# Folded weights dealt product by product into the attention of the first image

## The chip, the cores and the metric

The kernel runs on one core of a Trainium2 chip. The metric is the device time of one execution in microseconds. Before the change three runs took 2604.94, 2607.56 and 2609.03 us; the median is 2607.56 us. Engine names in the profile: PE is TensorE (matrix products), PEld its weight loads, DVE is VectorE, ACT is ScalarE, POOL is GpSimd, SP is the engine whose queue issues most DMAs.

## The reference, cut to what matters

Two layers over 8 images of 512 channels and 32 x 32 points (1024 tokens).

```
# layer 0: group norm, q/k/v, 8 heads of 64 channels
q = fake_quant(q); k = fake_quant(k); v = fake_quant(v)     # 8 bits, one range for all images
w = softmax(einsum('bct,bcs->bts', q * scale, k * scale))
a = einsum('bts,bcs->bct', w, v)
x = x + proj_w @ a + proj_b
# layer 1: group norm, attention with one head of 512 channels
qk = (t @ wq.T + bq) @ (t @ wk.T + bk).T / sqrt(512)
out = softmax(qk) @ (t @ wv.T + bv)
x = x + (out @ wp.T + bp)
```

Layer 1 has only one head, so its four weight matrices can be multiplied in pairs before any image is seen: wq with wk, and wv with wp. The kernel calls this the folding. It saves two of the four products with the tokens of each image. The biases that belong to it are folded along.

## The kernel before, in words

First comes a stage for all 8 images (0 to about 583 us): group norm and the products for q, k and v, written to DRAM, with the minimum and maximum that the quantization needs. Then `attention()` and layer 1 run over the images. `attention()` is a generator that hands out score tiles. A unit `u` is one score tile: image `b`, pair of heads `j` (4 pairs), half of the queries `hf` (2), block of keys `s` (8), so 64 units for each image, 16 for each pair.

For each unit, `scores(u)` makes the score tile `st` on TensorE: two products, one for each head of the pair, each over 64 of the 128 rows of the array, at the same time. ScalarE takes the exponential into `pt`. `ps_s` holds two score tiles, so the products of a tile wait until the exponential of the tile two places before has been taken. `split(u)` then divides `pt` into two float16 parts, `two`: the rounded value (a cast on ScalarE, GpSimd or VectorE) and the difference (VectorE). In the first image every fourth tile is *plain*: its exponential goes to `aside` and stays float32. `over_keys` multiplies the parts with the values (`av`), in four strips of 32 columns that run at the same time; for a plain tile in float32 with the values `vf`, in two strips of 64 columns. `totals` makes the row sums (`sm`) with a matrix of ones. The order on TensorE for four units `u` to `u+3` is: scores of `u+6` and `u+7`; values and sums of `u` and `u+1`; scores of `u+8` and `u+9`; values and sums of `u+2` and `u+3`. Each such round is one step of the generator (`advance()`).

When the last round of a pair's half is done, `finish` copies the values (`ao`) and the sums (`rs`) out of PSUM on ScalarE. After the second half the sums go out by DMA (`apart`), VectorE takes reciprocals (`rcs`), these go to DRAM and back spread over the partitions (`rs_d`, `rs`), and VectorE divides `ao`. There is one buffer for `rs`, so the sums of the next pair are copied after the division of this one. `load_pair` fetches the raw q, k and v of the next pair through two `raw` buffers, and VectorE quantizes them.

`fold()` is a second generator. It makes the folded weights: two times (`wn_h` into `wa`, `wn_v` into `wm`) four output blocks (`e`) of four products (`d`) each, every product 128 x 128 by 128 x 512 in float32, accumulated in one PSUM bank of `ps_o`, which ScalarE copies out. `through(i)` makes the bias column on VectorE (four reductions into `room`, a sum, four widenings into `wide`), `weigh` multiplies it with the weights (`wt_f`, four products 32 wide, then a copy on ScalarE), and `by_channel` gives the column sums (`wc_f`, four products with one column). At the end VectorE makes sums and differences of the blocks of `wa` and `wm`, and `wm` is stored to DRAM (`wm_d`) for the later images. Then the projection's weights (`load_wp`) and the first image's x (`load_x2`, tile `h`, which takes over the buffer of `wn_h`) are loaded.

In the kernel before, a loop over `fold()` decides the order: it adds up a weight for each yield of the folding (4.0 for a block of four products) and a weight for each round of attention, and takes rounds of attention while they are behind in proportion. TensorE thus gets four products in a row, then about two rounds of attention.

On TensorE all products are chained in the order of the program (`mm`, line 206). On the other engines, in this stage, the order within a queue comes from the scheduler of the tile framework; from the first image's projection on (`InOrder.planned`) it is chained as well. An engine works through its queue in order, and so does SP's DMA queue.

Of the kernel before, what the change touches and what calls it, by code (L numbers as in the profile page):

```python
# [15 lines left out]
ALU = mybir.AluOpType  # L16
# [3 lines left out]
B, C, HH, WW = 8, 512, 32, 32  # L20
T = HH * WW
CC = C // P
# [36 lines left out]
def attn_pair_kernel(  # L59
# [101 lines left out]
    def awaits(t):  # L161

        pe.t = max(pe.t, t + 0.1)
# [140 lines left out]
    with ExitStack() as fast:  # L304
        wts = fast.enter_context(tc.tile_pool(name="wts", bufs=1))
        def pair_ps(name):
            return ps_s.tile([P, 2, 512], F32, tag="s", name=name)
# [657 lines left out]
        def attention():  # L965
# [13 lines left out]
            def scores(u):  # L979
                b, j, hf, s = units[u]  # L980
                if hf == 0 and s == 0:
                    settle("qk")
                nm = f"{b}_{j}_{hf}"
                qt, kt, _ = pairs[b, j]
                st = pair_ps(f"st_{nm}_{s}")
                awaits(st_free[-2])
                for i, r in enumerate(HALF):
                    mm(
                        st[:, i, :], lhsT=kt[r, bass.ts(s, P)],
                        rhs=qt[r, bass.ts(hf, 512)], start=True, stop=True,  # L990
                    )
                if u >= 4:
                    need(u - 4)
                if plain(b, s):
                    pt = aside[:, u // 4 % 3].rearrange("p (i k) n -> p i (k n)", i=2)
                else:
                    pt = ptp.tile([P, 2, 512], F32, tag="p", name=f"pt_{nm}_{s}")
                there = act.do(
                    1.12, lambda: act.activation(pt, st, AF.Exp, scale=esc),
                    max(pe.t + 0.25, ready.get(u - 4, 0.0) + 0.1),  # L1000
                )
                st_free.append(there)
                pts[u] = pt, there
# [34 lines left out]
            def over_keys(us):  # L1038
                need(us[-1])
                awaits(ready[us[-1]])  # L1040
                pe.t += 0.12
                for u in us:
                    b, j, hf, s = units[u]
                    if s == 0:
                        avs[b, j, hf] = av_bank(f"av_{b}_{j}_{hf}")
                    if plain(b, s):
                        for i, r in enumerate(HALF):
                            mm(
                                avs[b, j, hf][r, :], lhsT=vfs[j][:, s // 4, r],
                                rhs=parts[u][:, i, :], start=False, stop=(s == NT - 1),  # L1050
                            )
                        continue
                    for w in range(2):
                        for i in range(4):
                            r = slice(i * QUAD, (i + 1) * QUAD)
                            mm(
                                avs[b, j, hf][r, :], lhsT=pairs[b, j][2][:, s, r],
                                rhs=parts[u][:, w, i // 2, :], start=(s == 0 and w == 0),
                                stop=(s == NT - 1 and w == 1),
                            )  # L1060
# [57 lines left out]
            for u in (0, 2, 4):  # L1118
                for i in (u, u + 1):
                    scores(i)  # L1120
                    split(i)
                yield 9.0 if u else 0.0, 0
            for u in range(0, len(units), 4):
                b, j, hf, s = units[u]
                if hf == 0 and s == 0:
                    n = b * PAIRS + j + 1
                    if n < B * PAIRS:
                        pairs[divmod(n, PAIRS)] = load_pair(*divmod(n, PAIRS))
                    settle("qv")

                def two(what, v):
                    if v < len(units):
                        what(v)
                        what(v + 1)

                pe.t += 0.12
                if not late:  # L1140
                    two(scores, u + 6)
                if late:
                    over_keys((u, u + 1))
                    two(scores, u + 6)
                    totals((u, u + 1))
                    over_keys((u + 2, u + 3))
                    totals((u + 2, u + 3))
                    two(split, u + 6)
                    two(scores, u + 8)
                elif dense:  # L1150
                    over_keys((u, u + 1))
                    totals((u, u + 1))
                    two(split, u + 6)
                    two(scores, u + 8)
                    over_keys((u + 2, u + 3))
                    totals((u + 2, u + 3))
                else:
                    over_keys(range(u, u + 4))
                    totals(range(u, u + 4))
                    two(split, u + 6)  # L1160
                    two(scores, u + 8)
                if s == NT - 4:
                    finish(b, j, hf)
                two(split, u + 8)
                pe.t += 0.15
                last = (j, hf, s) == (PAIRS - 1, NH - 1, NT - 4)
                yield 6.0 + (hf == NH - 1 and s == NT - 4), b + last

        xts, sums, wms, wps, mvs = {}, {}, {}, {}, {}

        def load_x2(b, dma):

            xts[b] = l1p.tile([P, CC, T], F32, tag="h", name=f"h2_{b}")
            for hf in range(NH):
                dma(xts[b][:, :, bass.ts(hf, 512)], x_v[b, :, :, bass.ts(hf, 512)])

        def load_wp(b, dma):
            wps[b] = l2p.tile([P, CC, C], F32, tag="sums", name=f"wp0_{b}")
            dma(wps[b], w_sq[WP0])
# [482 lines left out]
        def fold():  # L1662
# [16 lines left out]
            def through(i):  # L1679
                w, _, col = ((NQ1, NK1, V_BQ), (NV1, WP1, V_BV))[i]  # L1680
                z = small.tile([P, CC], F32, tag="z", name=f"z{i}")
                for e in range(CC):
                    dve.tensor_tensor_reduce(
                        room, wn[w][:, e, :], row, 1.0, 0.0, ALU.mult, ALU.add,
                        accum_out=z[:, e : e + 1],
                    )
                dve.tensor_add(z, z, vec[:, col : col + CC])
                widen(wide[:, i], z)

            for i, (rows, lw, rw) in enumerate(((wa_rows, NQ1, NK1), (wm_rows, NV1, WP1))):  # L1690
                through(i)
                for e in range(CC):
                    ps = bank(f"fold_{lw}_{e}")
                    for d in range(CC):
                        mm(
                            ps, lhsT=wn[lw][:, d, bass.ts(e, P)], rhs=wn[rw][:, d, :],
                            start=(d == 0), stop=(d == CC - 1),
                        )
                    act.copy(rows(e), ps.rearrange("p (a n) -> p a n", a=2))
                    yield 4.0  # L1700
            for i, (dst, w) in enumerate(((gb, NK1), (ob, WP1))):
                by_channel, _ = weigh(
                    bank, room, lambda e, w=w: wn[w][:, e, :], wide[:, i], f"f{i}"
                )
                yield 1.0
                tot = by_channel()
                if i == 0:
                    dve.tensor_copy(dst, tot)
                else:
                    dve.tensor_add(dst, tot, vec[:, V_BP : V_BP + CC])  # L1710
            a11, a12, a21, a22, s1, s2, s4 = (wa[:, i] for i in range(7))
            tt(s1, a21, a22, ALU.add)
            tt(s2, s1, a11, ALU.subtract)
            tt(a21, a11, a21, ALU.subtract)
            tt(s4, a12, s2, ALU.subtract)
            (m11, m12), (m21, m22), (v1, v2), (v3, v4) = ([t[:, i] for i in range(2)] for t in wm)
            tt(v1, m11, m12, ALU.subtract)
            tt(v2, m22, v1, ALU.subtract)
# [31 lines left out]


        att = attention()
        A_IMAGE = PAIRS * (NH * NT * 1.5 + 1.0)
        F_FOLD = 4.0 * 8 + 2.0
        F_FIRST = 4.0
        pos, done = 0.0, 0
        dense = True
        late = False

        def advance():  # L1760
            nonlocal pos, done
            step = next(att, None)
            pos, done = (math.inf, B) if step is None else (pos + step[0], step[1])

        def others():
            steps = None
# [5 lines left out]

        folded = 0.0
        for w in fold():
            folded += w
            while pos < (folded - F_FIRST) * A_IMAGE / F_FOLD:
                advance()
        load_wp(0, nc.sync.dma_start)  # L1780
        load_x2(0, nc.sync.dma_start)
        while done < 1:
            advance()

        for _ in range(LEAD):
            advance()
# [370 lines left out]
```

## Time and profile before

| | |
|---|---|
| profiled execution, device time | 2605.78 us |
| its span, from the first to the last instruction | 2604.0 us |
| instructions | 38580 |
| TensorE busy | 2532.2 us, 97% of the span |
| VectorE busy | 1905.0 us, 73% |
| ScalarE busy | 1358.1 us, 52% |
| GpSimd busy | 194.1 us, 7% |
| mean granted TensorE clock | 0.995 |
| folding, first and last product | 583.1 us to 675.4 us |
| projection of the first image, first product | 736.73 us |

The page gives the share of each engine in the whole span; the stage of the first image's attention is some 6% of it. Its timeline lists instructions in order of time, merged where the same operation follows itself: start, duration, engine, line of the kernel, operation, output and inputs, shape, count, and in brackets how long the engine stood idle before it and what ended that. Line 206 is the helper that records every product and line 91 the one that records VectorE and ScalarE work, so the tile names tell the operations apart. Durations of products are those of a pipeline; the steps from start to start tell what TensorE can do.

### The profile page before, as it was taken

What the parts mean: (1) busy time and instruction counts of PE and PEld (TensorE: products, weight loads), DVE (VectorE), ACT (ScalarE), POOL (GpSimd) and SP (SyncE); (2) the same over time, 40 slices, a digit from 0 to 9 for tenths busy, and PEclk for the clock granted to TensorE, in tenths of its full rate; (3) what the DMA queues carried; (4) which work ended last, traced back from release to release, by engine and by line L of the source; (5) the groups of instructions that cost most, each with busy time, mean ns of one, the idle gap of its engine ahead of it and who ended that gap; (6) DMA issues with size and microseconds to landing.
All of it is one profiled execution on the core that took longest, in us unless ns stands there. A gap on an engine that the chain in (4) does not pass through costs nothing.

```text
span 2604.0 us, 38580 instructions
## 1 busy us (share of the span) xinstructions
PE 2532.2 (97%) x15606; PEld 1750.0 (67%) x15606; DVE 1905.0 (73%) x2748; ACT 1358.1 (52%) x1696; POOL 194.1 (7%) x153
## 2 busy tenths in 40 slices
PE   8899999998889999999999999999999999999998
PEld 4688888872236775775677577757766775777687
DVE  7877777668767777877877787778777777775544
ACT  3222222217866674766566566746665665664121
POOL 0000000001110001000100010010001000100000
PEclk9999999999999999999999999999999999999999
DMA  5433333333321223223212322322232123212211
GB/s 183 152 127 122 117 117 118 125 131 104 123 66 54 58 94 115 65 74 112 92 49 75 123 93 63 98 89 79 86 102 98 49 78 118 86 47 88 86 37 38
DMA packets 156012, 243.07 MB, mean 93 GB/s; under 512 B 26544, under 2 KB 93104, under 8 KB 154288
## 3 DMA queue, kind: packets, MB, share of 16 engines
q1 hardware_dynamic: 125264, 182.81, 21.4%
q10 hardware_dynamic: 30560, 57.71, 6.5%
q8 instruction: 124, 2.03, 0.3%
q14 instruction: 64, 0.52, 0.1%
HBM read 153.64 MB, written 86.28 MB: 92 GB/s over the span
## 4 chain that ended last, share of the span: by engine, by line
PE 85%; DVE 4%; ACT 3%; issue 2%; DMA 2%; POOL 0%; SPq 0%; ACTq 0%; DVEq 0%
PE s L206 15%; PE o L206 14%; PE qkps L206 11%; PE pj L206 9%; PE av L206 8%; PE v2ps L206 7%; PE g L206 7%; PE vps L206 5%; PE st L206 4%; PE sm L206 4%; ACT pt L91 1%; PE fold L206 1%; DVE two L91 1%; ACT aside L91 0%; DVE acc L91 0%
## 5 line engine op out<-in xcount | busy, mean ns | idle before, releaser
L91 ACT ACTIVATE pt<-st,esc 128x1024 f32<-128x1024 f32 x496 | 527.0, 1114 | 344.1 <-PE st L206 323.7
L91 DVE TENSOR_TENSOR two<-pt,two 128x1024 f16<-128x1024 f32 x496 | 596.8, 1219 | 134.0 <-POOL two L1021 106.5
L91 ACT CAST two<-pt 128x1024 f16<-128x1024 f32 x358 | 362.2, 1055 | 7.9 <-issue 5.3
L1021 POOL CAST two<-pt 128x1024 f16<-128x1024 f32 x128 | 171.3, 1338 | 1546.2 <-ACT pt L91 769.3
L206 PE MATMUL av<-two,v 128*32 128x512 f16 x3968 | 245.0, 381 | 0.0
L206 PE MATMUL s<-g,h 128*128 128x256 f32 x1024 | 233.4, 380 | 0.0
L206 PE MATMUL pj<-ao,wp 128*128 128x512 f32 x512 | 224.7, 597 | 0.0
L206 PEld LDWEIGHTS s<-g,h 128*128 128x128 f32 x1024 | 193.0, 190 | 30.9 <-issue 4.3
L206 PE MATMUL st<-q,k 64*128 64x512 bf16 x1024 | 163.8, 382 | 25.3 <-ACT pt L91 13.1
L206 PEld LDWEIGHTS <-v 128*32 128x32 f16 x3968 | 91.2, 96 | 136.6 <-issue 63.2
L206 PEld LDWEIGHTS pj<-ao,wp 128*128 128x128 f32 x512 | 96.6, 191 | 122.3 <-issue 112.5
L206 PE MATMUL s<-g,sums 128*128 128x256 f32 x768 | 178.4, 381 | 0.2 <-DVE p L91 0.2
L91 ACT ACTIVATE u_ring<-qkps,qkbt 128x512 f32<-128x512 f32 x89 | 60.8, 684 | 224.3 <-PE qkps L206 224.3
L206 PE MATMUL o<-p,v 128*128 128x256 f32 x768 | 175.2, 382 | 1.0 <-DVE p L91 1.0
L206 PEld LDWEIGHTS o<-p,v 128*128 128x128 f32 x768 | 144.3, 190 | 27.0 <-issue 5.7
L206 PEld LDWEIGHTS s<-g,sums 128*128 128x128 f32 x768 | 144.7, 190 | 24.2 <-issue 4.6
L206 PE MATMUL sm<-two,ones 128*32 128x512 f16 x1984 | 136.7, 381 | 1.8 <-ACT rs L91 1.8
L206 PEld LDWEIGHTS <-k 64*128 64x128 bf16 x1024 | 34.8, 94 | 147.9 <-issue 144.5
L206 PE MATMUL qkps<-half,w_high 128*128 128x512 f32 x480 | 132.6, 399 | 0.0
L206 PE MATMUL qkps<-half,w_low 128*128 128x512 f32 x480 | 131.3, 396 | 0.5 <-DVE half L91 0.5
L206 PE MATMUL qkps<-half,w_mix 128*128 128x512 f32 x480 | 130.5, 394 | 1.1 <-DVE half L91 1.1
L206 PE MATMUL g<-h,wa 128*128 128x256 f32 x512 | 121.2, 385 | 1.6 <-DVE h L91 1.6
(219 smaller groups left out, 3836.2 us busy)
## 6 DMA issues: line engine op xcount, KB each, us to landing
rs<-rs_d SPq DMA_DIRECT2D x80, 256.0 KB
x<-in_x_dram SPq DMA_DIRECT2D x32, 512.0 KB
q_d<-wa SPq DMA_DIRECT2D x32, 512.0 KB
k_d<-wa SPq DMA_DIRECT2D x32, 512.0 KB
raw<-q_d SPq DMA_DIRECT2D x32, 512.0 KB
v_d<-v_ring SPq DMA_DIRECT2D x32, 512.0 KB
raw<-k_d SPq DMA_DIRECT2D x32, 512.0 KB
x_d<-h SPq DMA_DIRECT2D x64, 256.0 KB
```

Source lines behind the costliest of these rows:

```text
L91: ins = self.latest = op(*args, **kw).ins
L206: ins = nc.tensor.matmul(ps, lhsT=lhsT, rhs=rhs, **kw).ins
L1021: copy(two[:, 0], pt)
```

## The change

The products of the folding are dealt singly. `fold()` now yields after every product instead of after every block of four, and `scores(u)` takes one step of it ahead of each odd unit of the first image. Nine steps (two blocks and one product) run before the attention begins. The loop with its weights is gone, and the generators yield no weights any more.

Within `fold()` the order changes: `through(i)` stands behind the last block of its half instead of ahead of the first; the bias products of the first half (`weigh`, `by_channel`) follow directly, together with the sums and differences of `wa` and the two loads `load_wp` and `load_x2`, all ahead of the second half. The second half's bias products, the differences of `wm` and its stores come at the end.

In `over_keys`, the values of a plain tile are taken in four strips of 32 columns instead of two of 64.

```diff
@@ def scores(u)
                 st = pair_ps(f"st_{nm}_{s}")
+                if b == 0 and u % 2 == 1:
+                    next(folding, None)
                 awaits(st_free[-2])
@@ def over_keys(us)
                     if plain(b, s):
-                        for i, r in enumerate(HALF):
+                        for i in range(4):
+                            r = slice(i * QUAD, (i + 1) * QUAD)
                             mm(
                                 avs[b, j, hf][r, :], lhsT=vfs[j][:, s // 4, r],
-                                rhs=parts[u][:, i, :], start=False, stop=(s == NT - 1),
+                                rhs=parts[u][:, i // 2, :], start=False, stop=(s == NT - 1),
                             )
@@ def attention()
-                yield 9.0 if u else 0.0, 0
+                yield 0
...
-                yield 6.0 + (hf == NH - 1 and s == NT - 4), b + last
+                yield b + last
@@ def fold()
             for i, (rows, lw, rw) in enumerate(((wa_rows, NQ1, NK1), (wm_rows, NV1, WP1))):
-                through(i)
                 for e in range(CC):
                     ps = bank(f"fold_{lw}_{e}")
                     for d in range(CC):
                         mm(
                             ps, lhsT=wn[lw][:, d, bass.ts(e, P)], rhs=wn[rw][:, d, :],
                             start=(d == 0), stop=(d == CC - 1),
                         )
+                        if d + 1 < CC:
+                            yield
                     act.copy(rows(e), ps.rearrange("p (a n) -> p a n", a=2))
-                    yield 4.0
-            for i, (dst, w) in enumerate(((gb, NK1), (ob, WP1))):
+                    if e == CC - 1:
+                        through(i)
+                    yield
+                dst, w = ((gb, NK1), (ob, WP1))[i]
                 by_channel, _ = weigh(
                     bank, room, lambda e, w=w: wn[w][:, e, :], wide[:, i], f"f{i}"
                 )
-                yield 1.0
+                yield
                 tot = by_channel()
                 if i == 0:
                     dve.tensor_copy(dst, tot)
+                    a11, a12, a21, a22, s1, s2, s4 = (wa[:, i] for i in range(7))
+                    tt(s1, a21, a22, ALU.add)
+                    tt(s2, s1, a11, ALU.subtract)
+                    tt(a21, a11, a21, ALU.subtract)
+                    tt(s4, a12, s2, ALU.subtract)
+                    yield
+                    load_wp(0, nc.sync.dma_start)
+                    load_x2(0, nc.sync.dma_start)
                 else:
                     dve.tensor_add(dst, tot, vec[:, V_BP : V_BP + CC])
-            a11, a12, a21, a22, s1, s2, s4 = (wa[:, i] for i in range(7))
-            tt(s1, a21, a22, ALU.add)
-            tt(s2, s1, a11, ALU.subtract)
-            tt(a21, a11, a21, ALU.subtract)
-            tt(s4, a12, s2, ALU.subtract)
@@ the order of the generators
         att = attention()
-        A_IMAGE = PAIRS * (NH * NT * 1.5 + 1.0)
-        F_FOLD = 4.0 * 8 + 2.0
-        F_FIRST = 4.0
-        pos, done = 0.0, 0
+        done = 0
...
         def advance():
-            nonlocal pos, done
-            step = next(att, None)
-            pos, done = (math.inf, B) if step is None else (pos + step[0], step[1])
+            nonlocal done
+            done = next(att, B)
...
-        folded = 0.0
-        for w in fold():
-            folded += w
-            while pos < (folded - F_FIRST) * A_IMAGE / F_FOLD:
-                advance()
-        load_wp(0, nc.sync.dma_start)
-        load_x2(0, nc.sync.dma_start)
+        folding = fold()
+        for _ in range(9):
+            next(folding)
         while done < 1:
             advance()
+        for _ in folding:
+            pass
```

## The prediction

> **What bounds the kernel now.** I read the share of busy time first (TensorE 97% of the span), then the busy times by stretch, then the timeline of the one stage that the change touches, 583 to 737 us, engine by engine. Columns of the stretches: length, busy time and instructions of TensorE, weight load, VectorE, ScalarE, GpSimd, granted clock, DMA share, GB/s.
>
> ```profile
> 595.60:602.40 6.80, 4.58 (x8) 1.72 (x8) 6.76 (x7) 5.83 (x6) 1.12 (x1) 0.50 0.29 84
> ...
> 604.31:619.59 15.28, 14.43 (x114) 4.30 (x114) 13.12 (x15) 12.17 (x14) 3.29 (x2) 1.00 0.12 39
> 619.59:635.13 15.54, 14.50 (x115) 4.36 (x114) 13.46 (x15) 12.54 (x15) 2.90 (x2) 1.00 0.24 69
> ...
> 698.34:736.73 38.39, 30.84 (x322) 8.92 (x321) 31.35 (x33) 36.56 (x39) 11.06 (x6) 0.98 0.29 84
> ```
>
> While folding goes on, eight score tiles take 15.5 us with TensorE nearly always busy; once it is over (last row), ScalarE is busy 36.6 of 38.4 us and sets the pace. The timeline of TensorE shows the start, and how eight tiles are made up:
>
> ```profile
> 593.53 0.39 PE L206 MATMUL st<-q,k 64*128 64x512 bf16 x2 [0.99 <-ACT pt L91]
> 594.53 0.39 PE L206 MATMUL st<-q,k 64*128 64x512 bf16 x2 [0.61 <-ACT pt L91]
> 597.43 0.61 PE L206 MATMUL st<-q,k 64*128 64x512 bf16 x2 [2.50 <-ACT pt L91]
> 598.43 0.61 PE L206 MATMUL st<-q,k 64*128 64x512 bf16 x2 [0.40 <-ACT aside L91]
> 598.97 5.41 PE L206 MATMUL fold<-wn_h 128*128 128x512 f32 x8
> 604.31 0.61 PE L206 MATMUL st<-q,k 64*128 64x512 bf16 x4
> 604.85 1.05 PE L206 MATMUL av<-two,v 128*32 128x512 f16 x16
> 605.72 0.61 PE L206 MATMUL sm<-two,ones 128*32 128x512 f16 x8
> 606.26 0.39 PE L206 MATMUL st<-q,k 64*128 64x512 bf16 x2
> 607.07 0.39 PE L206 MATMUL st<-q,k 64*128 64x512 bf16 x2 [0.42 <-ACT aside L91]
> 607.39 0.62 PE L206 MATMUL av<-two,v 128*32 128x512 f16 x8
> 607.94 1.08 PE L206 MATMUL av<-aside,vf 128*64 128x512 f32 x4
> 608.95 0.40 PE L206 MATMUL sm<-two,ones 128*32 128x512 f16 x4
> 609.17 1.03 PE L206 MATMUL sm<-aside,ones 128*32 128x512 f32 x4
> 610.13 3.70 PE L206 MATMUL fold<-wn_h 128*128 128x512 f32 x8
> 613.76 0.61 PE L206 MATMUL st<-q,k 64*128 64x512 bf16 x4
> ```
>
> A score tile is two records (x2), a product of the folding two, because float32 goes through twice. Two things are to be seen. The second score tile of a pair often waits for an exponential (0.42 here), since only two score tiles fit in PSUM. And four products in a row, 610.13 to 613.76, hold TensorE for 3.63 us, in which ScalarE runs dry, as its own timeline says:
>
> ```profile
> 600.74 1.04 ACT L91 CAST two<-pt 128x1024 f16<-128x1024 f32 x1
> 604.41 0.58 ACT L91 COPY wa<-fold 128x512 f32<-128x512 f32 x1 [2.64 <-PE fold L206]
> ```
>
> TensorE waits for ScalarE in one part of each round, ScalarE for TensorE in the other. All that follows 737 us stands in the same order on every engine of the changed kernel, so what this stage gains or loses goes to the end as it is.
>
> **The change, part by part.**
>
> *The stalls, removed.* An unstalled pair of score tiles takes 604.31 to 604.85, 0.54; the stalled one 606.26 to 607.39, 1.13: a stall of 0.59. The next half round has the longer form, 621.61 to 622.93, 1.32, plus 0.07 ahead of it: 0.85. So 1.44 per eight tiles. One product now stands ahead of every odd tile, the very place of the wait, and it is longer than the wait. I checked the exponentials against the new spacing: the exponential two tiles back starts when its tile is done and takes 1.0; between that and the odd tile lie at least 1.41 (values and sums of a pair) + 0.22 + a product of about 1, some 2.6 us. ScalarE's work, 12.5 per eight tiles in the second stretch, stays below the new 14.6 of TensorE. I cost the remaining stall at nothing; if ScalarE were late after all, each 0.1 us per odd tile would cost 2.3.
>
> *The products, moved.* Record by record in the trace, the eight records of a group start 0.43 apart, except 0.53 after the first and 0.53 from the last to the next score tile; the steps between operations with the same form of tile lack that tenth (values to values 0.215, scores to values 0.31). A single product thus costs 0.53 + 0.53 = 1.06, and the pair of score tiles split by it 0.09 more (0.31 in place of 0.22): 1.14 against 3.63/4 = 0.91 in a group. No trace row shows a product alone between score tiles. From below, two records at 0.43 are 0.86; from above, if neither weight load (0.19 by its rows) were hidden, 1.52. I take 1.14, the step of a group's own first and last record, which have the same neighbours.
>
> The Trainium skill, "TensorEngine Tiling (Array Packing)", Key Properties, says that a change of the tiling mode, other than a change of tile, makes TensorE drain. It speaks against dealing products singly, since each one brings two such changes; the trace agrees, with 0.31 against 0.215 per change, and that tenth is in the 1.14 already.
>
> *The values of the plain tile.* Four products 32 wide replace two 64 wide. Before: 0.31 into them, 0.47 between, 0.52 out. The bias products (wt, four 32 wide, float32) show 0.43 between, and neighbours of the same width 0.215 in and 0.43 out. Gain 0.235 per four tiles, between 0 and 0.31. It counts only where TensorE sets the pace.
>
> *Sum from the first values product (604.85) to score tile 54 (698.34), 93.5 us before.* Four tiles without stalls cost 604.31 to 606.26, 1.95, plus 606.26 to 610.13 less 0.59, 3.28: 5.23. After: twelve such groups at 5.23 - 0.235 = 59.9, less 0.54 for tiles 6 and 7 that lie ahead; 23 odd tiles each with a product, or with one of the four bias steps that I price alike (in before 1.00, 690.45 to 691.45, and 0.98, 689.47 to 690.45): 23 x 1.14 = 26.2. Together 85.6: 7.9 saved.
>
> *The start.* ScalarE's first two exponentials and casts end at 596.25 as before, the next three exponentials at 599.3. In the new order the copy of a fold (0.48 from start to start), a cast (0.95) and the exponential of tile 5 (1.0) end near 601.8; tile 7 follows and the values product at 602.2 instead of 604.85: 2.65 saved, with one product more already done (hence 23, not 24). But the clock row above says 0.50 from 595.6 to 602.4, where the four products took 5.35 instead of 3.63; with products at twice 1.06 the same chain ends near 603.4, and 1.4 is left. I take 1.9.
>
> The Trainium skill, "TensorE: Matmul & The Clock Gate", Part 1, says that the clock falls to half after an idle window of about 3.4 us. By that rule products dealt into the gaps of the start could keep the clock up, which would make the 2.65 the better figure; no trace here shows that.
>
> *VectorE.* The bias work of the second fold (four reductions at 0.68, a sum, four widenings: about 3.6) moves from 585 to 594, where it lay among the first quantizations, into tiles 14 to 24, behind the copy of gb, which waits for TensorE's column sums. VectorE is busy 13.12 + 13.46 = 26.6 in the first two stretches; with 3.6 more it has 30.2 in two new rounds of 29.3. It runs behind by one to five us (the 4.2 it idles there are waits for raw tiles at the head of its queue). Behind it wait the quantizations of pair 2, needed only at tile 32, and the differences `two`, needed about seven tiles after their scores; the third stretch leaves it 5 us to catch up. I take 1.6 lost, between 0 and 5.
>
> *DMA.* The two loads of h (1 MB each) leave at tile 17 instead of 688.82, ahead of pair 2's values and pair 3's queries on SP; the wm stores take their old place before the last pair's chain. In before, next to the h loads, raw<-q_d took 6.2 and raw<-k_d 5.7 instead of 5.0 and 3.7. Hidden by the same look-ahead; without it, 3 us. The stall at 711.5 to 713.2 (ScalarE waits for the division of the pair before) I leave: 0, up to 1.75 gained.
>
> Sum: 7.9 + 1.9 - 1.6 = 8.2. The profiled execution took 2605.78 with a span of 2604.0; the median of the runs is 2607.56, 1.8 above, so 2607.56 - 8.2 = 2599.4.
>
> **Rivals.** (1) *The price of dealing eats the gain.* If a weight load is left open at each product, it costs 1.33 to 1.52: 23 x 0.19 = 4.4 to 8.7 lost, 2603.8 to 2608.1. For it: a group's first record shows a tenth that nothing else explains. Against: in groups 0.19 of load is hidden under 0.43.
> (2) *VectorE becomes the bound in pairs 0 and 1.* The full 5 us are lost: 2602.8, and 2605 if the h loads delay the raw tiles too. For it the 30.2 of 29.3; against it the long lead of its results.
> (3) *Slower: the chain of the row sums.* ScalarE can't copy the sums of a new pair before the old pair's division. This chain (sums out, reciprocal, back by DMA, division) took 11.8 us from 636.0 and 14.2 from 698.3, where DMA was full; a round is now 14.6 in place of 15.5, and pair 3's keys now stand inside the first chain on SP. If it took 18.5, three pairs would each wait 3.9: 11.7 - 8.2 = 3.5 lost, 2611. It turns into a loss from 17.4 on.
> (4) *It doesn't deal as said.* The order of the changed kernel's instructions shows a product ahead of each odd tile, so this is nearly out: 2607.6.
>
> **How the numbers follow.** Forecast 0.66, rival 1 0.11, rival 2 0.12, rival 3 0.08, rival 4 0.03. Predicted 2599.4. The low end takes the 2.65 of the start, no loss on VectorE and the 1.75 of the late stall, 12.3, and a little of a cheaper product: 2594. The high end, 2607, takes in rival 2 and most of rival 1, and leaves out rival 3. A change under 0.2% (5.2 us) can't be told from none. Below 2602.3 lie the forecast and a little of rival 2: 0.70 faster; 0.20 within; 0.10 slower.
>
> **What would show it.** Eight tiles with folding at 14.6 us in place of 15.5; no wait of st for aside or pt between 604 and 690; single products at 1.06 from start to the next score tile; 0.43 out of the plain tile's values; the first values product near 603; the projection (pj) starting near 728.5 instead of 736.7. I am wrong if products take 1.3 or more, if waits of av for `two` by VectorE appear between tiles 16 and 32, or if ScalarE waits for ao at each pair.

## The result, and the profile after

The changed kernel takes 2597.56 us (median of 7 runs, 2596.45 to 2598.81), the kernel before 2606.03 us in the same comparison (7 runs, 2603.55 to 2609.03): ratio 0.9968, 95% interval 0.9958 to 0.9978. That is 8.5 us less; the forecast was 8.2 less than 2607.56, or 2599.4. The profiled executions have spans of 2604.0 and 2595.8 us, but 1.5 of these 8.2 us had already appeared when the first folding product started (583.14 and 581.67), ahead of everything that the change touches. So the stages are compared below by their own lengths, not by their times of day.

The stretches of the kernel before, from the first folding product to the first values product, from there to score tile 54 (the first after the folding), and from there to the projection (columns as in the prediction: length, busy time of TensorE, weight load, VectorE, ScalarE and GpSimd, granted clock, DMA share, GB/s); the last of the three was shown there:

```profile
583.14:604.85 21.71, 15.52 (x41) 5.73 (x42) 20.18 (x50) 11.96 (x13) 1.84 (x2) 0.84 0.57 194
604.85:698.34 93.49, 86.64 (x696) 26.90 (x694) 73.48 (x79) 75.97 (x86) 16.58 (x12) 1.00 0.34 109
```

The same three of the changed kernel:

```profile
581.67:601.34 19.67, 16.22 (x42) 5.53 (x43) 16.91 (x37) 12.39 (x14) 1.71 (x2) 0.91 0.63 214
601.34:686.74 85.40, 85.40 (x742) 27.23 (x740) 75.00 (x90) 76.58 (x84) 19.89 (x12) 1.00 0.37 116
686.74:727.61 40.87, 30.91 (x339) 10.08 (x337) 33.63 (x36) 36.74 (x42) 9.57 (x6) 0.96 0.28 84
```

The middle stretch falls from 93.49 to 85.40, and in it TensorE is now busy for 85.40 of 85.40 us: nothing is left there but its own work. The start gives 2.04, although one product of the folding more lies in it: 13 instead of 12 stand ahead of the first values product, so about 1 us of the 8.1 that the middle stretch loses is moved work, as the prediction had counted. The last stretch, in which ScalarE has the most work (36.6 and 36.7 us), is 2.48 us longer: ScalarE idles 4.1 us in it instead of 1.8. Of this, 3.07 instead of 1.16 us lie ahead of one copy of row sums, and a new wait of 0.74 us for a score tile (at 709.83) follows a stretch at half clock (704.7 to 708.1). A second profile of the changed kernel has 19.13, 85.40 and 39.80. From the first folding product to the projection that is 153.6 us before, and 145.9 and 144.3 after: 7.7 and 9.3 less, around the 8.5 of the medians.

TensorE's timeline of half a round with folding in the changed kernel:

```profile
621.35 0.39 PE L206 MATMUL st<-q,k 64*128 64x512 bf16 x2
621.67 1.12 PE L206 MATMUL fold<-wn_v 128*128 128x512 f32 x2
622.73 0.39 PE L206 MATMUL st<-q,k 64*128 64x512 bf16 x2
623.05 1.05 PE L206 MATMUL av<-two,v 128*32 128x512 f16 x16
623.92 0.60 PE L206 MATMUL sm<-two,ones 128*32 128x512 f16 x8
624.46 0.39 PE L206 MATMUL st<-q,k 64*128 64x512 bf16 x2
624.78 1.12 PE L206 MATMUL fold<-wn_v 128*128 128x512 f32 x2
625.84 0.39 PE L206 MATMUL st<-q,k 64*128 64x512 bf16 x2
626.15 0.62 PE L206 MATMUL av<-two,v 128*32 128x512 f16 x8
626.60 1.03 PE L206 MATMUL av<-aside,vf 128*32 128x512 f32 x8
627.46 0.39 PE L206 MATMUL sm<-two,ones 128*32 128x512 f16 x4
627.67 1.03 PE L206 MATMUL sm<-aside,ones 128*32 128x512 f32 x4
628.63 0.39 PE L206 MATMUL st<-q,k 64*128 64x512 bf16 x2
```

No line carries a wait. A single product takes 1.06 from its start to the next score tile (621.67 to 622.73). The plain tile's values in four strips take 0.86 (626.60 to 627.46), two passes of 0.43. Four tiles take 7.28, eight 14.56. TensorE's waits by releaser between 585 and 800 us, of the kernel before (engine, what waited, what it waited for: total, times, longest) ...

```profile
PE st L206 <- ACT pt L91: 10.6, 12, 2.5
PE st L206 <- ACT aside L91: 7.3, 15, 0.6
```

... and of the changed one:

```profile
PE st L206 <- ACT pt L91: 10.3, 14, 2.1
...
PE st L206 <- ACT aside L91: 1.8, 3, 0.6
```

In the middle stretch before, 12 waits for `aside` took 6.1 us; they are gone, and the three that are left lie in the last stretch. The waits for `pt` lie outside the middle stretch in both kernels.

### The profile page after: what moved, and what is told of

The parts are those of the page before. It is cut to its first block, busy times and chain, and to the rows that moved or that the text cites. A ratio compares the mean times of both kernels' runs of the same rounds, so it can differ in the third digit from the quotient of the medians.

```text
span 2595.8 us, 38704 instructions
## 1 busy us (share of the span) xinstructions
PE 2531.0 (98%) x15670; PEld 1751.0 (67%) x15670; DVE 1902.8 (73%) x2748; ACT 1359.9 (52%) x1696; POOL 196.4 (8%) x153
## 4 chain that ended last, share of the span: by engine, by line
PE 83%; DVE 6%; DMA 2%; ACT 2%; issue 2%; POOL 0%; SPq 0%; ACTq 0%; DVEq 0%
PE s L206 15%; PE o L206 13%; PE qkps L206 12%; PE pj L206 8%; PE av L206 7%; PE v2ps L206 7%; PE g L206 6%; PE vps L206 6%; PE st L206 4%; PE sm L206 3%; DVE two L91 2%; ACT pt L91 1%; DMA rs<-rs_d 1%; DVE h L91 1%; DVE acc L91 0%
## 5 line engine op out<-in xcount | busy, mean ns | idle before, releaser
L206 PEld LDWEIGHTS o<-p,v 128*128 128x128 f32 x768 | 144.3, 190 | 27.1 <-issue 5.7
```

The source lines that it names most:

```text
L206: ins = nc.tensor.matmul(ps, lhsT=lhsT, rhs=rhs, **kw).ins
```

## The experiments

Stages of all kernels in their profiles, us, worked out from the starts of the first product of each stage. "Half clock" are the times between the first folding product and 740 us in which the granted clock was half, start and length. The ratio is to the kernel before.

| kernel | start | middle | last | sum | half clock | ratio, 95% interval |
|---|---|---|---|---|---|---|
| before | 21.71 | 93.49 | 38.39 | 153.6 | 595.6 6.8, 735.6 3.4 | 1 |
| changed | 19.67 | 85.40 | 40.87 | 145.9 | 595.5 3.4, 704.7 3.4 | 0.9968, 0.9958 to 0.9978 |
| quads | 21.96 | 91.06 | 38.40 | 151.4 | 592.9 10.2, 712.3 3.4 | 0.9989, 0.9979 to 0.9998 |
| strips64 | 19.68 | 88.59 | 37.93 | 146.2 | 596.6 3.4 | 0.9971, 0.9960 to 0.9982 |
| fours | 21.12 | 91.26 | 38.00 | 150.4 | 594.5 6.8, 731.0 3.4 | 0.9990, 0.9980 to 1.0000 |
| even | 17.44 | 87.29 | 43.16 | 147.9 | 705.0 6.8 | 0.9974, 0.9965 to 0.9984 |
| bias_early | 20.35 | 85.40 | 40.42 | 146.2 | 705.9 3.4 | 0.9974, 0.9963 to 0.9986 |
| stores_late | 18.87 | 85.68 | 41.08 | 145.6 | 705.3 3.4 | 0.9964, 0.9950 to 0.9979 |
| rs_two | 18.87 | 85.42 | 40.75 | 145.0 | 722.3 3.4 | 0.9972, 0.9961 to 0.9984 |
| div_late | 18.87 | 85.40 | 38.34 | 142.6 | none | 0.9962, 0.9948 to 0.9976 |
| strips64_rs_two | 19.68 | 88.59 | 38.50 | 146.8 | 597.3 3.4 | 0.9969, 0.9957 to 0.9982 |
| div_only | 19.46 | 85.40 | 41.60 | 146.4 | 598.5 3.4, 704.3 6.8 | 0.9968, 0.9957 to 0.9979 |
| after_five (changed again) | 19.13 | 85.40 | 39.80 | 144.3 | 598.8 3.4, 704.7 3.4 | 0.9971, 0.9959 to 0.9983 |
| div_late_five | 18.87 | 85.40 | 39.01 | 143.3 | 724.9 3.4 | 0.9966, 0.9952 to 0.9979 |

**Which part of the change gains: quads and fours.** In quads, the kernel before has only the four strips of the plain tile's values (the second part of the diff). In fours, the changed kernel takes its products four in a row again:

```diff
-                if b == 0 and u % 2 == 1:
-                    next(folding, None)
+                if b == 0 and u % 8 == 6:
+                    for _ in range(4):
+                        next(folding, None)
...
-        for _ in range(9):
+        for _ in range(8):
             next(folding)
```

> The kernel before with one part of the change alone: the values of the plain tiles in four strips of 32 columns, products still dealt four at a time. Theory (the two changes of tile form around the 64 wide strips cost TensorE 0.235 us per four tiles, and TensorE sets the pace where folding goes on): eight tiles with folding take 15.54 - 0.47 = 15.07 us, and the stretch from the first values product to score tile 54 falls from 93.5 to about 90.7; whole kernel 2.8 us faster. Rival (ScalarE's exponentials set the pace in the half round without products, and the shorter values only lengthen the wait of the score tiles): the stretch stays within 1 us of 93.5, and the waits of st for aside grow by what the values lose.

> The changed kernel with the dealing alone undone: eight steps of the folding ahead of the attention and then four in a row ahead of every eighth score tile; the new places of the bias work, the loads and the stores and the four strips stay. Theory (the gain is the stalls of the second score tile, 1.44 us per eight tiles, less 0.94 for products that stand alone, and the start): eight tiles with folding take about 15.1 us instead of 14.56, waits of st for aside and pt of 0.4 to 0.6 come back twice per eight tiles, the start loses about 2 us again, whole kernel about 5 us slower than the changed one. Rival (the gain comes from the new places of the bias work and the loads): the stretch from the first values product to score tile 54 stays within 1 us of 85.4 and the kernel within 1.5 us of the changed one.

The strips alone take the middle stretch from 93.49 to 91.06, 2.4 less (whole kernel 2603.43 us, the kernel before 2606.45). With the dealing undone and all else kept, it is 91.26, 5.9 more than in the changed kernel (whole kernel 2603.43 us again, the kernel before 2606.45), and the waits that the prediction named are back, in fours' view of waits from 585 to 800 us:

```profile
ACT wa L91 <- PE fold L206: 18.6, 4, 10.9
...
PE st L206 <- ACT aside L91: 7.5, 16, 0.6
```

Of the 18.6 us, 10.9 are one wait at the start that the kernel before and the changed one have too; the other three waits are ScalarE's for four products in a row. In the middle stretch of fours score tiles wait 12 times for `aside`, 5.6 us, and in the changed kernel never.

So with the strips in place the dealing takes 5.7 us off the stretch (91.06 to 85.40), and without them 4.9 (93.49 to the 88.59 of strips64, next); the strips take 2.4 off alone and 3.2 with the dealing in place. About 1 us of the dealing's share is the product that has moved into the start. quads and fours differ by 0.2, so the new places of the bias work, the loads and the stores bring nothing in this stretch.

**The strips undone in the changed kernel: strips64.**

```diff
-                        for i in range(4):
-                            r = slice(i * QUAD, (i + 1) * QUAD)
+                        for i, r in enumerate(HALF):
...
-                                rhs=parts[u][:, i // 2, :], start=False, stop=(s == NT - 1),
+                                rhs=parts[u][:, i, :], start=False, stop=(s == NT - 1),
```

> The changed kernel with the values of the plain tiles put back to two strips of 64 columns, products dealt singly. Theory: eight tiles with folding take 14.56 + 0.47 = 15.03 us, the stretch from the first values product to score tile 54 goes from 85.4 to about 88.2, whole kernel 2.8 us slower than the changed one. Rival (there is slack on TensorE once the products are dealt singly): the stretch stays within 1 us of 85.4.

The middle and last stretch of strips64:

```profile
602.31:690.90 88.59, 88.59 (x693) 25.66 (x692) 77.96 (x94) 77.33 (x84) 18.53 (x12) 1.00 0.35 114
...
690.90:728.83 37.93, 30.36 (x322) 8.92 (x320) 32.02 (x33) 36.88 (x40) 10.15 (x6) 1.00 0.30 86
```

TensorE is fully busy here too, and 3.2 us longer (88.59; the theory said 88.2). Yet the whole kernel is level with the changed one (2598.55 us, overlapping intervals), since the last stretch is 2.9 us shorter. What the strips gain in the middle is given back in the last stretch: why was the open question of the runs that follow.

**A product ahead of the even tiles: even.** The condition in the diff becomes `u % 2 == 0 and u > 0`, so that a product separates each pair of tiles from the values.

> The changed kernel with each product ahead of the even score tile, so that the two score tiles of a pair stand together again. Theory of the place (a product helps because it stands exactly where the odd tile waits): the product still lies between an exponential and the tile that needs it, so most of the wait stays covered (1.41 + 1.06 + 0.22 = 2.69 us against two exponentials, 2.1), a product costs 0.09 less because the pair isn't split, and the stretch from the first values product to score tile 54 falls from 85.4 to about 83.3. Rival (only a product between the two tiles of a pair covers the wait, because ScalarE takes the two exponentials of a pair one after the other and casts stand between them): waits of st for pt or aside of 0.2 to 0.5 per pair come back, 24 to 27 of them, and the stretch takes 88 or more.

The start is 2.2 us shorter and the middle 1.9 longer, together the same within 0.3; the gain that I expected did not come. About 1 us of both is one product, which lies behind the first values product here and ahead of it in the changed kernel. TensorE idles 2.2 us in the middle stretch, 1.0 of it for copies of row sums and 1.15, in three waits, for exponentials; 87.29 is neither the 83.3 of the theory nor the 88 or more of its rival. The last stretch is the longest of all, 43.16, with a half clock of 6.8 us in it: the sums of pair (0,2) leave SP's queue 3.5 us after their copy (688.16, 691.68), behind the load of raw keys, and the chain takes 16.9 us. Ahead of the odd or of the even tile is thus the same to the first two stretches.

**VectorE's bias work back at the start: bias_early.** Both `through(i)` stand ahead of the first product again.

> The changed kernel with the bias reductions of both halves on VectorE ahead of all products again, as in the kernel before. Prediction's step on VectorE (their 3.6 us in tiles 14 to 24 leave VectorE behind and cost 1.6 us, up to 5): the stretch from the first values product to score tile 54 falls from 85.4 to 84 or less. Rival, by the trace of the changed kernel (no wait of TensorE for VectorE's differences in that stretch): it stays at 85.4 within 0.5, and the start gets 0.3 to 1.5 us longer, since the reductions stand among the first quantizations again.

Its middle stretch:

```profile
602.78:688.18 85.40, 85.40 (x740) 27.22 (x739) 74.00 (x80) 77.13 (x84) 18.32 (x12) 1.00 0.38 124
```

85.40, to the hundredth what the changed kernel has: the bias work cost TensorE nothing in this stretch. The start, 20.35, is 0.7 to 1.2 us longer than in the two profiles of the changed kernel, as the rival said, though no half clock falls into it. Its 2599.11 us is not distinguishable from the changed kernel.

**The chain of the row sums, three tries: stores_late, rs_two, strips64_rs_two.** In the last stretch ScalarE waited 3.07 us for a division, as its timeline of the changed kernel shows:

```profile
698.48 1.05 ACT L91 CAST two<-pt 128x1024 f16<-128x1024 f32 x1
702.60 0.59 ACT L91 COPY rs<-sm 128x512 f32<-128x512 f32 x1 [3.07 <-DVE ao L91]
```

and VectorE itself for the sums that come back by DMA:

```profile
694.99 4.27 DVE L91 TENSOR_TENSOR two<-pt,two 128x1024 f16<-128x1024 f32 x3
701.24 1.29 DVE L91 SCALAR_TENSOR_TENSOR ao<-ao,scl,rs 128x1024 f32<-128x1024 f32 x1 [1.98 <-DMA rs<-rs_d]
```

From the end of the sums' copy to the end of the division the chain took 14.8 us here (687.75 to 702.52), against 14.3 before (698.30 to 712.57). stores_late moves the stores of `wm` behind the attention, in case their DMA slows the chain. rs_two gives the last pair's `rs` a buffer of its own, from the pool of `ao`:

```diff
-                    rss[b, j] = l1p.tile([P, NH, 512], F32, tag="rs", name=f"rs_{nm}")
+                    apart_rs = (b, j) == (0, PAIRS - 1)
+                    rss[b, j] = (aop if apart_rs else l1p).tile(
+                        [P, NH, 512], F32, tag="ao" if apart_rs else "rs", name=f"rs_{nm}"
+                    )
```

strips64_rs_two is rs_two with the strips of strips64.

> The changed kernel with the four stores of the second half's folded weights (2 MB) issued after the first image's attention instead of in the middle and at tile 54. Theory A (DMA traffic of the stores makes the row-sum chain of the third pair slow: its broadcasts leave at 696.58 and VectorE waits for them till 701.24): the chain gets 1 to 2 us shorter, from 14.8 to 13 or so, and the late part takes 39 to 40 us instead of 40.87. Theory B (the chain is long because the last keys' load and VectorE's queue stand ahead of it, not because of the stores, which are over by then): chain and late part stay within 0.5 us.

> The changed kernel with a second buffer for the row sums of the first image's last pair (taken from the pool of the attention outputs), so that ScalarE's copy of these sums no longer waits for the division of the pair before. Theory (the changed kernel's late part, 40.87 us from score tile 54 to the projection against 38.39 before, is long because the chain of the row sums, 14.8 us, no longer fits into eight tiles): the wait of sm for rs, 2.74 us, goes away, and with it the half clock from 704.7 on; the late part takes 37 to 38 us, the kernel is 3 to 4 us faster than the changed one, near 2594. Rival (ScalarE's own work sets the pace of the late part, and the wait only stands in for its other waits): the late part stays above 39.5.

> The same second buffer, with the plain tiles' values in two strips of 64 columns again. Theory (the 3.2 us that the four strips save up to tile 54 were given back to the chain of the row sums, so that the kernel with 64 wide strips came out level): with the chain out of the way the four strips are worth their 3 us in the whole kernel: this one reaches tile 54 3 us later than the one with the second buffer alone, takes the same 37 to 38 us from there, and is 2 to 3 us slower as a whole. Rival (the four strips are worth nothing in the end, whatever the chain does): both start the projection within 1 us of each other.

stores_late: the last stretch is 41.08 and the chain 14.8, nothing changes; 2598.07 us. rs_two: ScalarE's wait for this division is gone, and the last stretch is still 40.75; 2599.2 us. My theory that the buffer alone costs the time fell. The number is the one that its rival gave, above 39.5, but what is left is not ScalarE's own work: a new wait stands there. strips64_rs_two: 2599.2 us, last stretch 38.50; its sum is 1.7 us longer than that of rs_two, between the 2 to 3 of the theory and the 1 of the rival, and the medians are the same. Where the wait went in rs_two, ScalarE's timeline says:

```profile
699.68 0.59 ACT L91 COPY rs<-sm 128x512 f32<-128x512 f32 x1
...
705.29 1.11 ACT L91 ACTIVATE pt<-st,esc 128x1024 f32<-128x1024 f32 x1 [2.00 <-DVE two L91]
```

The sums are copied 2.9 us earlier, but 2.00 us are now lost in waiting for VectorE's difference `two`, which frees the buffer of `pt`. And VectorE was late because the division stood at the head of its queue and waited there, with the differences behind it:

```profile
695.37 4.26 DVE L91 TENSOR_TENSOR two<-pt,two 128x1024 f16<-128x1024 f32 x3
701.88 1.58 DVE L91 SCALAR_TENSOR_TENSOR ao<-ao,scl,rs 128x1024 f32<-128x1024 f32 x1 [2.24 <-DMA rs<-rs_d]
703.39 0.68 DVE L91 CAST two<-pt 128x1024 f16<-128x1024 f32 x1
```

Such a wait doesn't always cost its full length: in strips64_rs_two the division waits 2.50 us at the head of the queue (it starts at 704.51), and ScalarE loses only 0.35 behind it (at 707.87).

**Both waits at once, and one alone: div_late and div_only.** div_late is rs_two with the division of pair (0,2) held back and chained behind the differences of score tile 61, three places later in VectorE's queue; div_only has the later division without the second buffer.

```diff
-                    dve.later("ao", elements(1100), divide, dve.t + 7.0, 20.0)
+                    if (b, j) == (0, PAIRS - 2):
+                        held.append(divide)
+                    else:
+                        dve.later("ao", elements(1100), divide, dve.t + 7.0, 20.0)
...
                 two(split, u + 8)
+                if held and (j, hf, s) == (PAIRS - 1, 0, NT - 4):
+                    prior = dve.latest
+                    held.pop()()
+                    dve.after(prior)
```

> rs_two with the division of pair (0,2) three places later in VectorE's queue, behind the two of the score tiles 60 and 61, whose data are there while the sums come back; nothing else moves. In rs_two VectorE idles 2.24 us at the head of its queue for that division (703.5 its end) with these differences behind it, and ScalarE then waits 2.00 for one of them. Theory (what the late part loses is VectorE's wait at the head of its queue, with the chain of the row sums behind it): both waits go, and the 40.75 us from score tile 54 to the projection fall to 38.5 to 39.2; first folding product to projection 145.0 -> 142.8 to 143.5; whole time 1.5 to 2.2 us below rs_two. Rival (kernels that reach score tile 54 earlier carry a backlog of VectorE with them, 34.7 us of work in this part against 31.4 before, and whatever stands at the head of its queue is late by as much): the wait moves to another releaser, the late part stays above 40, the whole time as rs_two.

> The changed kernel with the division of pair (0,2) three places later in VectorE's queue, but with the one buffer of the row sums. Theory (two waits at one division have to go together: ScalarE's copy of the next pair's sums, and VectorE's differences behind the division): the division ends at 703.4 to 704 instead of 702.5, ScalarE waits 4.0 to 4.6 for it instead of 3.07, and the late part is 41 to 42.5 us instead of 40.87. Rival (VectorE's place alone decides, the buffer does nothing, as rs_two suggests by itself): the late part falls to 38.5 to 39.2.

VectorE in div_late, from its timeline, and the last stretch:

```profile
694.93 4.26 DVE L91 TENSOR_TENSOR two<-pt,two 128x1024 f16<-128x1024 f32 x3
699.12 0.68 DVE L91 CAST two<-pt 128x1024 f16<-128x1024 f32 x1
699.83 2.36 DVE L91 TENSOR_TENSOR two<-pt,two 128x1024 f16<-128x1024 f32 x2
702.11 2.06 DVE L91 SCALAR_TENSOR_TENSOR ao<-ao,scl,rs 128x1024 f32<-128x1024 f32 x1
```

```profile
687.04:725.38 38.34, 29.42 (x339) 9.85 (x337) 34.76 (x36) 36.39 (x40) 10.25 (x6) 1.00 0.31 92
```

The division starts 0.2 us later than in rs_two but has no wait ahead of it (it takes 2.06 us there instead of 1.58; why, no run shows), and the last stretch falls from 40.75 to 38.34, with VectorE as busy as in rs_two (34.8 against 34.7 us). The rival, a mere backlog of VectorE, would have kept it above 40. In div_only the last stretch is 41.60, in the range that the theory gave. The division ends where the theory put it (705.88, with tile 54 2.1 us later than in the changed kernel, so 703.8 on the clock of that kernel), but ScalarE's wait is not the 4.0 to 4.6 it named: the scheduler puts the copy two exponentials further back, and ScalarE waits 2.94 for the division, then 1.74 for a score tile, behind the start of 6.8 us at half clock (704.3); 2597.59 us. Either edit by itself gains nothing, both together gain 2.4 us of the last stretch in these profiles. A half clock of 3.4 us falls into the last stretch of rs_two (722.3) and none into that of div_late, but it isn't what makes the difference: from its last wait on, ScalarE takes 8.77 us to the same exponential in rs_two (718.88 to 727.65) and 8.78 in div_late (716.63 to 725.41).

**div_late beside the changed kernel on one chip: after_five and div_late_five**, the same two kernels, timed in five rounds.

> The changed kernel as it is, timed beside div_late_five on the same chip: 8.0 to 9.0 us below the kernel before by the runs so far (0.9965 to 0.9970); late part 40.5 to 41.

> The changed kernel with the second buffer of the row sums and the later division. If what the stage gains stays (145.9 -> 142.6 us from the first folding product to the projection in the profiles): 2 to 3.3 us below after_five, 0.9955 to 0.9960 of the kernel before. If the clock takes it back in what follows, as it did in the profiled run (the clock was at half for 6.8 us at 776): level with after_five within 1.5 us.

The changed kernel takes 2597.41 us (0.9971, 0.9959 to 0.9983), div_late 2595.44 us (0.9966, 0.9952 to 0.9979); div_late's first runs had 2594.97. In the profiles of this pair the gain is smaller than in the first: the last stretch 39.80 and 39.01, the sum 144.3 and 143.3 us. So div_late is faster than the kernel before, and its median is 1.97 us under the changed kernel's, just short of the 2 to 3.3 of my first case, but the intervals overlap: that it beats the changed kernel is likely and not settled.

## Why the prediction was right, and where it was not

*The stalls and the price of a single product: right.* Eight tiles at 14.56 (forecast 14.6), a product at 1.06, no wait of a score tile in the middle stretch; quads and fours show that it is the dealing that takes the wait away. The middle stretch was forecast at 85.6, with VectorE's 1.6 to come on top, and is 85.4. Rival 1 (a weight load left open) fell with the 1.06.

*The plain tile: right.* 0.86 instead of two strips with 0.47 between; the forecast of 0.235 for four tiles gives 2.8 in twelve groups, and the runs bracket it with 2.4 (quads) and 3.2 (strips64).

*The start: right in size.* Forecast 1.9, between 1.4 and 2.65; 2.04 and 2.58 in the two profiles of the changed kernel. The two ends were the half clock and the full one, and both occur: 19.67 and 19.13 with 3.4 us of half clock, 18.87 without any, in stores_late, rs_two and both profiles of div_late. That last is 2.84 saved, a little over the upper figure.

*VectorE: wrong.* "I take 1.6 lost, between 0 and 5" was sized by VectorE's lag, and a lag costs only what TensorE waits for. TensorE waited for nothing: 85.40 busy of 85.40, the same as in bias_early, where the work lies at the start. The lag came: in the second round of the changed kernel, 615.9 to 630.5, VectorE is busy 14.53 of 14.60 us, and from a score tile's product to the end of its difference it takes 6.5 to 8.3 us in tiles 16 to 24, against 4.3 to 5.3 in the kernel before. But these differences still end 3.9 to 6.7 us ahead of the values products that read them (differences and values products paired in their order). The step that failed is the one from "it runs behind" to "TensorE loses by it"; the lead, which the prediction itself named, covered all of it. Rival 2 fell.

*The late stall: wrong.* "I leave: 0, up to 1.75 gained" was a loss of 1.4 to 2.5 us. The prediction had the chain of the row sums in its rival 3, and set 17.4 us as the length from which it turns into a loss; its remark that DMA was full in the chain from 698.3 doesn't hold, since the DMA engines' share there is 0.24. The chain grew only from 14.3 to 14.8; what the prediction had not compared is when ScalarE comes to the copy that waits for it. In the changed kernel that is 11.8 us after the last copy (702.60 less 3.07, less 687.75), before 13.1 (712.60 less 1.16, less 698.30). Part of this is the order of ScalarE's own queue, which the scheduler made anew: in the kernel before an exponential of 1.0 us stands ahead of the copy, in the changed one behind it. strips64 shows the old order, with 12.6 us to the copy and a chain of 13.4:

```profile
703.33 1.11 ACT L91 ACTIVATE pt<-st,esc 128x1024 f32<-128x1024 f32 x1
705.31 0.59 ACT L91 COPY rs<-sm 128x512 f32<-128x512 f32 x1 [0.87 <-DVE ao L91]
```

So 3.07 of wait in place of 1.16 are 0.5 of a longer chain and 1.4 of an earlier copy. In the second profile of the changed kernel the chain is 14.0, shorter than before, and the wait is still 2.69, since ScalarE comes to the copy after 11.4 us: the earlier copy is the part that both profiles show. quads, with the old order, keeps 38.40, and the changed kernel, bias_early and stores_late, with the new one, lie between 39.8 and 41.1 (fours has the new one too, but two copies of the folding ahead of the copy, and 38.00). That the order alone would do it was not tried: even has the old order, but a chain of 16.9 us, and is the worst. What div_late shows is that the loss goes with the waits at this division on both engines: wholly in the first pair of profiles (40.87 to 38.34, before 38.39), and 0.8 of 1.4 us in the second (39.80 to 39.01). The half clock that follows the wait probably adds its part: in the five profiles in which one begins between 704.7 and 705.9 (changed, after_five, bias_early, stores_late and, the longest, even) ScalarE waits 0.6 to 2.0 us for score tiles soon after, and in strips64 and div_late, which have none there, it doesn't. Of the signs of being wrong that the prediction named, one came in part: ScalarE waits for `ao` in more than one place, 1.00 us at 673.26 as well, where TensorE loses nothing by it.

The two wrong terms, 1.6 lost that was not and 1.4 to 2.5 lost that was not foreseen, cancelled by luck; so the difference came out at 8.5 for 8.2 with two of its parts off.

What stays open: what in the change made the scheduler move the copy, and how much of the rest of the difference between single profiles is the half clock behind 740 us, which falls differently from one execution to the next (3.4 us at 735.6 and at 790.2 before, 6.8 us at 779.8 in the changed kernel). None of the runs held it fixed.

## What to carry to other kernels

When small products are to fill the waits of another chain, deal them singly, each longer than the wait (here 1.06 us against 0.4 to 0.6); in a group they fill one wait and starve the engine that feeds the next. Whether a product stood ahead of the first or of the second tile of a pair made no difference here to the start and the middle stretch together. Where a scheduler sets the order of the other engines' queues, compare these orders in the stage behind the change too: here a copy that moved ahead of one exponential, with a chain about as long as before (14.0 and 14.8 us, before 14.3), went with a loss of 1.4 to 2.5 of the 10 to 11 us gained. And of a chain of fixed length (here sums out, reciprocal, back by DMA, division) compare the length with the time at which its waiter arrives, not with the average round. An instruction that waits for a DMA at the head of a queue delays what stands behind it as well: a second buffer for one of those who waited showed nothing here until the instruction had been moved too.

## What the runs showed of the hardware

The clock can fall to half without one long idle time of TensorE. Two stretches of 3.4 us ahead of a drop, and the drop, in the changed kernel:

```profile
588.67:592.08 3.41, 2.87 (x11) 0.73 (x9) 1.36 (x6) 3.24 (x4) 0.00 (x0) 1.00 0.85 277
592.08:595.50 3.42, 1.56 (x6) 0.41 (x5) 3.35 (x5) 3.42 (x4) 0.00 (x0) 1.00 0.17 58
595.50:598.90 3.40, 3.13 (x8) 0.73 (x7) 3.40 (x4) 2.71 (x4) 1.31 (x1) 0.50 0.89 269
```

and in the kernel before, where a stretch with a little over half is followed by one at full clock:

```profile
588.78:592.19 3.41, 1.72 (x8) 0.53 (x7) 3.41 (x9) 1.87 (x2) 0.00 (x0) 1.00 0.27 109
592.19:595.60 3.41, 1.13 (x8) 0.25 (x5) 2.77 (x11) 3.24 (x4) 0.00 (x0) 1.00 0.86 297
595.60:602.40 6.80, 4.58 (x8) 1.72 (x8) 6.76 (x7) 5.83 (x6) 1.12 (x1) 0.50 0.29 84
```

In the fourteen profiles there are 36 drops between 585 and 800 us, of 3.4, 6.8 or 10.2 us, all on one grid of 3.41 us in each profile. In 27 of them no single idle time of TensorE that reaches into the 3.41 us ahead is as long as 3.41 us; the shortest such longest idle time is 1.09 us. In the windows ahead of the drops TensorE was busy for 0 to 1.71 us, up to half. Of the windows of this grid at full clock, all with up to 1.53 us of busy time were followed by half clock and none with 1.72 or more; in between both occur (6 drops, 9 windows without one), so busy time as the profile has it does not decide these. Once at half clock, windows with up to 2.72 us of busy time were followed by half clock again, and those with 2.85 or more by the full one. The Trainium skill, "TensorE: Matmul & The Clock Gate", Part 1, tells of an idle window of about 3.4 us. The length agrees, but by these figures the window need not be idle.

It fits this that of the profiles with the dealing of the changed kernel, whose gaps at the start are partly filled, some show a drop there and some none, at 0.3 to 0.8 us of difference; where the edges of the windows fall may decide it, which no run here set apart.
